# An LSTM over 512 steps: the x products of the last steps as one-level Strassen pairs, with the weight sums on GpSimd

## The chip, the cores and the metric

One core of one Trainium2 chip. The metric is the device time of the whole program in microseconds (us): median of three runs before the change 3068.2 us (3067.43 to 3068.24). One further execution was recorded by the hardware profiler; the traces below are of that one. Engines: PE is TensorE, DVE is VectorE, ACT is ScalarE, POOL is GpSimd, SP issues the DMAs.

## What is computed

```
xW = einsum('ntd,dg->ntg', x, Wx) + b           # x: 32 x 512 x 512, Wx: 512 x 2048
def step(carry, xw_t):
    a = xw_t + prev_h @ Wh                       # Wh: 512 x 2048
    i, f, o = sigmoid(first three quarters of a); g = tanh(last quarter)
    next_c = f * prev_c + i * g
    next_h = o * tanh(next_c)
out = x + hs
```

All of it is float32. Each of the 512 steps needs the h of the step before; the x products of a step need nothing of the recurrence and can be made at any earlier time.

## The kernel before

**A step.** The 32 rows of the batch sit in 32 of PE's columns, and four column groups (j = 0 to 3) work side by side on four quarters of the gates. `h_part` (line 544) multiplies h by Wh: in the steps up to 468 it takes 16 matmuls of 512 columns, from step 469 on (`SPLIT`) 32 of 256 columns, since the units are then treated as two halves. Its order in a split step is half 0 with the first two k, half 1 with the first k, half 0 with the last two, half 1 with the last three, where the first two k are the h of half 0, the last two that of half 1. So half 0 is complete after 20 of 32 matmuls. `cell` (line 557) then runs for each half: ACT takes the sigmoids and the tanh out of PSUM (`s`, `o`), DVE multiplies (`prod`), adds (`s`, which holds c), ACT takes tanh (`tanh_c`), DVE multiplies by o (`hbuf`) and transposes into `ht`, which the next step's matmuls read. The chain of half 0 is called chain A in the prediction. At the end of `cell` the residual sum `oc` (x plus h, 128 columns) is made on POOL, on DVE in the last eight steps. `seed_step` copies the x products of the next step into its PSUM banks on ACT, ahead of the step's `cell`.

**The x products.** Steps 0 to 17 are made early. The 480 steps 18 to 497 come in 15 groups of 32, through a fast scheme (26 block products for a 4x4 split, with a Strassen level inside each), whose block products are streamed between the h parts; DVE adds them up (`w_op`, 1024 columns each) and SP stores and reloads them through `xwd`. The last stream matmuls are in step 467; sums of the last group (`w_op`, one in a step) go on until step 476.

**The last 14 steps** (498 to 511) are plain products. For each step there are 16 units (four chunks of x times four quarters q of the columns); a unit is four matmuls of 128 columns, and two neighbouring units of a half are issued as four of 256. They fill PE behind the h part: 11 units in step 467, 13 in step 468, 5 in each of the steps 469 to 508, none in 509 to 511. When a step's 16 units are done, DVE adds the bias and moves the bank to SBUF (128x512). Lines 1240 to 1245 and 1395 to 1412 hold this; `plain_part` (line 485) issues one unit or two. The raw weights that they read are loaded again late (`late_loads`, steps 452 to 467).

The order of the instructions in steps 0 to 19 comes from a planner that lists recorded operations by due times; from step 20 on (`nc.flush()`) each engine gets its instructions in the order in which the code is written. An engine runs them in that order.

Of the kernel before, what the change touches and what calls it, by code (L numbers as in the profile page):

```python
# [13 lines left out]
P = 128  # L14
B = 32
T = 512
NJ = 4
# [4 lines left out]
W = G * P  # L22
HW = G * H

HEAD = 18
GS = 32
NG = 15
TAIL = T - HEAD - NG * GS
# [11 lines left out]
END = HEAD + GS * NG - AHEAD  # L40
SPLIT = END + 2
# [63 lines left out]
class Plan:  # L105
# [57 lines left out]
    def add(self, engine, op, call, out, ins):  # L163
        if not self.live:
            call()
            return
        self.ops.append((engine, op, call, out, ins))
# [219 lines left out]
def kernel(  # L387
# [10 lines left out]
    nc = Plan(tc.nc)  # L398
    add, sub = nc.vector.tensor_add, nc.vector.tensor_sub
# [6 lines left out]
    xbank = [psum.tile([P, W], F32, name=f"xbank_{i}") for i in range(5)]  # L406
# [24 lines left out]
    def buf_of(i):  # L431
        if i < NC:
            return cbuf[:, i]
        return spare if i == NC else r1[:, i - NC + 1]
# [22 lines left out]
    def x_plain(t):  # L457
        if 2 * TC <= t < HEAD:
            return xnat[:, 2, t % TC]
        return x_early[:, t % TC] if T - TAIL <= t < T - TC else x_of(t)  # L460
# [5 lines left out]
    def raw(blk):  # L466

        if late_weights[0]:
            return late_r[:, LATE_AT[blk]] if blk < 6 else late_more[blk - 6]
        return r1[:, blk]  # L470
# [14 lines left out]
    def plain_part(t, c, q, n, bank):  # L485

        ko, ki = divmod(c, 2)
        a = q % 2 * P
        for j in range(NJ):
            nc.tensor.matmul(  # L490
                bank[j * B : (j + 1) * B, q * P : (q + n) * P],
                x_plain(t)[:, c],
                raw(ko * 4 + j)[:, 2 * ki + 1 - q // 2, a : a + n * P],
                start=c == 0 and q == 0,
                stop=True,
                skip_group_check=True,
            )
# [121 lines left out]
    def take(pool):  # L619
        assert pool, "no buffer left"  # L620
        return pool.pop(0)
# [396 lines left out]
    xw_late = {}  # L1018
# [125 lines left out]
    def keep(p, bias_in=False):  # L1144
# [12 lines left out]
        if p >= PARKED:  # L1157
            kept_stores.append(lambda: nc.sync.dma_start(out=kept[n], in_=dst))

    with tc.manual_schedule():  # L1160
        nc.vector.memset(tanh_c, 0.0)
        nc.vector.memset(sring[0], 0.0)
# [74 lines left out]
        }  # L1237

        HEAD_STEPS = STREAM0
        plain_tail = []  # L1240
        tail_banks = [xbank[2], xbank[3]]
        for p in range(TAIL):
            plain_tail += [(p, c, q) for c in range(4) for q in range(4)]
        plain_tail[8:24] = plain_tail[16:24] + plain_tail[8:16]
        late_halves = []

        for p in HEAD_PLAINS[0]:
            nc.scalar.copy(plain_bank(p), bias_full)

        for t in range(T):  # L1250
# [141 lines left out]
                late_loads.pop(0)()  # L1392
            emit_matmuls(n)
            load_v_ahead()
            kept_late = []
            due = 0 if t < END else max(0, 13 - n // 2) if t < SPLIT else 5
            while due and plain_tail:
                p, c, q = plain_tail[0]
                m = 2 if due > 1 and q % 2 == 0 else 1
                plain_part(HEAD + NG * GS + p, c, q, m, tail_banks[p % 2])  # L1400
                del plain_tail[:m]
                due -= m
                if c == 3 and q + m == 4:
                    kept_late.append(p)
            cell(t)
            for p in kept_late:
                if not late_halves:
                    late = buf_of(take(free_c))
                    late_halves += [late[:, 0:2], late[:, 2:4]]
                dst = late_halves.pop(0).rearrange("p s c -> p (s c)")  # L1410
                xw_late[HEAD + NG * GS + p] = dst
                add(dst, tail_banks[p % 2], bias_full)
            if t == T - 8:
                nc.vector.transpose(x_last, x_of(T - 1).rearrange("p q b -> p (q b)"))

# [49 lines left out]
```

## Time and profile before

| what | value |
|---|---|
| median of three runs | 3068.2 us (3067.43 to 3068.24) |
| profiled execution | 3067.07 us, span 3065.3 us |
| PE busy | 3055.8 us (100%) |
| DVE busy | 2339.0 us (76%) |
| ACT busy | 1466.3 us (48%) |
| POOL busy | 248.4 us (8%), 504 `oc` sums of 483 ns in the mean |
| PE in the chain that ended last | 99% |
| granted PE clock | 1.000 |

Times in the trace are counted from the start of the span. A row of the timeline gives start, length, engine, operation, out<-in and shapes, and in brackets how long the engine stood idle before it and what ended that. A window row gives for each engine busy time and number of records, then granted clock, DMA share and GB/s. Nearly all instructions carry line 125, that of the recording layer, so the tiles tell them apart. A float32 matmul leaves two records.

### The profile page before, as it was taken

The numbers are of one execution on the slowest core, as the hardware profiler recorded it, in microseconds if no ns is written. First come the engines' busy times: TensorE is split into PE (matmuls) and PEld (weight loads), VectorE is DVE, ScalarE is ACT, GpSimd is POOL, SyncE is SP. The second block draws the span as 40 slices with busy tenths as digits, with TensorE's granted clock in tenths as the row PEclk, the third lists the DMA queues.
The fourth block names the chain that finished last, engine by engine and source line by source line (L and its number), as shares of the span: only waits on it lengthen the run. The fifth ranks groups of instructions, "written<-read, shape, count | busy, mean of one in ns | idle before, by whom it ended". The sixth has DMA issues, their size and how long they took to land.

```text
span 3065.3 us, 108321 instructions
## 1 busy us (share of the span) xinstructions
PE 3055.8 (100%) x43688; PEld 1614.1 (53%) x43688; DVE 2339.0 (76%) x6312; ACT 1466.3 (48%) x5474; POOL 248.4 (8%) x511
## 2 busy tenths in 40 slices
PE   9999999999999999999999999999999999999999
PEld 6774444444445555555555555555555555555676
DVE  8678787787878878787787877878778787787644
ACT  1345445454444544544445454454544445454444
POOL 1000000000000000000000000000000000000110
PEclk9999999999999999999999999999999999999999
DMA  9988887787877878778787777777877787788530
GB/s 329 328 283 281 266 258 256 239 263 235 267 245 247 262 238 269 241 245 268 233 272 236 247 265 240 256 251 246 262 245 254 245 257 256 235 271 269 158 87 18
DMA packets 320436, 752.61 MB, mean 246 GB/s; under 512 B 52160, under 2 KB 104640, under 8 KB 319424
## 3 DMA queue, kind: packets, MB, share of 16 engines
q1 hardware_dynamic: 319936, 745.69, 75.4%
q8 instruction: 344, 5.64, 0.8%
q14 instruction: 156, 1.28, 0.1%
HBM read 564.34 MB, written 184.30 MB: 244 GB/s over the span
## 4 chain that ended last, share of the span: by engine, by line
PE 99%; DVE 1%; DMA 0%; SPq 0%; ACT 0%; issue 0%; ACTq 0%; DVEq 0%
PE gbank L125 55%; PE xbank L125 38%; PE bbank L125 6%; DMA vdram<-vring 0%; DVE xs L125 0%; DMA xnat<-in_x_dram 0%; DVE ubuf L125 0%; SPq L125 0%; DVE prod L125 0%; ACT s L125 0%; DVE s L125 0%; DVE xbank L125 0%; DVE hbuf L125 0%; ACT tanh_c L125 0%; DVE ht L125 0%
## 5 line engine op out<-in xcount | busy, mean ns | idle before, releaser
L125 PE MATMUL gbank<-wh_sb,ht 128*32 128x512 f32 (+1 forms) x16256 | 1772.2, 575 | 1.7 <-DVE ht L125 1.6
L125 PEld LDWEIGHTS gbank<-wh_sb,ht 128*32 128x32 f32 x16256 | 588.6, 110 | 840.6 <-issue 711.6
L125 ACT ACTIVATE s<-gbank 128x64 f32<-128x64 f32 (+2 forms) x1920 | 331.2, 257 | 1211.3 <-PE gbank L125 1210.7
L125 PE MATMUL xbank<-vring,ubuf 128*32 128x256 f32 (+1 forms) x13584 | 848.1, 368 | 0.0
L125 PEld LDWEIGHTS xbank<-vring,ubuf 128*32 128x32 f32 x13584 | 513.1, 110 | 305.1 <-issue 137.3
L125 DVE TENSOR_TENSOR prod<-s 128x128 f32<-128x128 f32 (+1 forms) x1007 | 290.7, 289 | 486.5 <-ACT s L125 481.9
L125 POOL TENSOR_TENSOR oc<-xnat,ht 128x128 f32<-128x128 f32 x504 | 243.3, 483 | 2745.4 <-DVE ht L125 1360.1
L125 ACT ACTIVATE tanh_c<-s 128x64 f32<-128x64 f32 (+1 forms) x1007 | 259.1, 257 | 238.7 <-DVE s L125 236.4
L125 DVE STREAM_TRANSPOSE ht<-hbuf 128x64 f32<-128x64 f32 (+1 forms) x1005 | 247.5, 246 | 72.6 <-DVE hbuf L125 0.9
L125 ACT COPY cbuf<-xbank 128x256 f32<-128x256 f32 (+1 forms) x679 | 281.9, 439 | 40.2 <-PE xbank L125 33.1
L125 ACT COPY gbank<-xw 128x512 f32<-128x512 f32 (+1 forms) x486 | 285.1, 589 | 3.6 <-DMA vring<-vdram 2.5
L125 DVE TENSOR_TENSOR s<-prod 128x64 f32<-128x64 f32 (+1 forms) x1007 | 227.5, 226 | 34.2
L125 DVE TENSOR_TENSOR hbuf<-o,tanh_c 128x64 f32<-128x64 f32 (+1 forms) x1007 | 209.2, 208 | 34.5 <-ACT tanh_c L125 33.7
L125 DVE TENSOR_TENSOR cbuf<-xbank,cbuf 128x256 f32<-128x256 f32 x452 | 176.5, 409 | 48.5 <-ACT cbuf L125 43.4
L125 DVE TENSOR_TENSOR cbuf<-cbuf 128x1024 f32<-128x1024 f32 x172 | 209.5, 1222 | 0.7
L125 PE MATMUL xbank<-vring,r 128*32 128x256 f32 (+1 forms) x3216 | 207.5, 357 | 0.0
L125 PE MATMUL xbank<-vring,xs 128*32 128x256 f32 (+1 forms) x3120 | 200.8, 356 | 0.0
L125 PE MATMUL bbank<-vring,ubuf 128*32 128x256 f32 (+1 forms) x2600 | 183.2, 342 | 0.0
L125 ACT COPY r<-xbank 128x256 f32<-128x256 f32 (+1 forms) x411 | 175.1, 439 | 15.8 <-PE xbank L125 13.7
L125 PEld LDWEIGHTS xbank<-vring,r 128*32 128x32 f32 x3216 | 120.6, 110 | 81.3 <-issue 47.4
L125 ACT ACTIVATE o<-gbank 128x128 f32<-128x128 f32 (+1 forms) x508 | 154.7, 305 | 0.0
L125 PEld LDWEIGHTS xbank<-vring,xs 128*32 128x32 f32 x3120 | 115.8, 110 | 62.6 <-issue 23.5
(128 smaller groups left out, 2120.3 us busy)
## 6 DMA issues: line engine op xcount, KB each, us to landing
vring<-vdram SPq DMA_DIRECT2D x310, 896.0 KB, 5.9
xw<-xwd SPq DMA_DIRECT2D x1920, 64.0 KB, 4.5
xwd<-cbuf SPq DMA_DIRECT2D x140, 512.0 KB, 4.5
xwd<-r SPq DMA_DIRECT2D x83, 512.0 KB, 4.7
out_dram<-oc SPq DMA_DIRECT2D x255, 128.0 KB, 3.8
xnat<-in_x_dram SPq DMA_DIRECT2D x62, 512.0 KB, 5.3
xs<-in_x_grouped_dram SPq DMA_DIRECT2D x45, 512.0 KB, 5.0
vring<-vdram SPq DMA_DIRECT2D x33, 512.0 KB, 5.1
```

Source lines behind the costliest of these rows:

```text
L125: self.plan.add(self.name, op, lambda: call(*args, **kw), out, rest)
```

## The change

Steps 499 to 510 are taken as six pairs. A pair is a 2x2 block product for each half ko of the depth: rows are the two steps, the depth is cut into two chunks, the columns into two halves of 256. Seven products (Winograd's form of Strassen) replace eight. Each product has four units, so a pair has 28 units where two plain steps had 32. Steps 498 and 511 stay plain, 16 units each. In all there are 200 units instead of 224.

- **Weight sums**: t1 = b12 - b11, t2 = b22 - t1, t3 = b22 - b12, n4 = b21 - t2 for each of eight blocks of weights, 256 columns each; `prepare` issues 1024 columns a step on POOL in the steps 468 to 475. They go into `ubuf` and a part of `vring`, which the stream no longer needs.
- **Sums of x** (`begin`): four POOL operations of 64 columns for each pair; ACT also copies the bias seed into the pair's bank.
- **Results**: products accumulate in PSUM so that a pair needs four ACT copies (begin 512, corners 2x256, right 256, finish 256 columns) and three DVE adds (top, right, low, 256 columns each). They stand behind the `cell` of the step in whose fill their last unit was issued.
- **Order**: `fill` takes units until the step's share is reached, or until a product needs a copy that is not yet issued; `share` spreads the paired units up to step 507 and the rest up to step 509. Units by step: 467: 8; 468: 13; 469: 5; 470: 2; 471: 5; 472: 3; 473 to 488: 5 each; 489 to 509: 4 each; 510 and 511: none.

POOL, from the residual sum of step 467 to that of step 471; before, only residual sums stand there (ht_95 and ht_96 are the h of even and odd steps, oc_97 and oc_98 the two result buffers):

```order
L125 TENSOR_TENSOR oc_98<-xnat,ht_96 128x128
L125 TENSOR_TENSOR oc_97<-xnat,ht_95 128x128
L125 TENSOR_TENSOR oc_97<-xnat,ht_96 128x128
L125 TENSOR_TENSOR oc_98<-xnat,ht_95 128x128
L125 TENSOR_TENSOR oc_98<-xnat,ht_96 128x128
```

And now, from the end of step 467 to the residual sum of step 470 (xs_79, cbuf and r_74 hold the raw weights, ubuf and vring the sums, seeds_own the x of steps 496 to 503):

```order
L125 TENSOR_TENSOR vring<-seeds_own 128x64
L125 TENSOR_TENSOR vring<-vring,seeds_own 128x64
L125 TENSOR_TENSOR vring<-seeds_own 128x64
L125 TENSOR_TENSOR vring<-seeds_own,vring 128x64
L125 TENSOR_TENSOR ubuf<-xs_79 128x2x256 x2
L125 TENSOR_TENSOR oc_97<-xnat,ht_95 128x128
L125 TENSOR_TENSOR ubuf<-xs_79 128x2x256
L125 TENSOR_TENSOR ubuf<-cbuf 128x256
L125 TENSOR_TENSOR vring<-r_74 128x256
L125 TENSOR_TENSOR oc_97<-xnat,ht_96 128x128
L125 TENSOR_TENSOR ubuf<-xs_79,ubuf 128x2x256 x2
L125 TENSOR_TENSOR oc_98<-xnat,ht_95 128x128
```

The four small sums of x of the first pair come first; then each step has its weight sums ahead of its own residual sum and behind that of the step before.

PE in step 507, before: the h part, then five units of the plain product of step 511 (four units as eight matmuls of 256 columns, one as four of 128), then the h part of step 508 (xbank_66 and xbank_67 hold the two halves of odd steps, gbank those of even ones):

```order
L125 MATMUL xbank_66<-wh_sb,ht_95 32x256 x8
L125 MATMUL xbank_67<-wh_sb,ht_95 32x256 x12
L125 MATMUL xbank_69<-xs_79,xnat 32x256 x6
L125 MATMUL xbank_69<-cbuf,xnat 32x256
L125 MATMUL xbank_69<-r_74,xnat 32x256
L125 MATMUL xbank_69<-xs_79,xnat 32x128 x2
L125 MATMUL xbank_69<-cbuf,xnat 32x128
L125 MATMUL xbank_69<-r_74,xnat 32x128
L125 MATMUL gbank_72<-wh_sb,ht_96 32x256 x8
```

And now, the same place:

```order
L125 MATMUL xbank_66<-wh_sb,ht_95 32x256 x8
L125 MATMUL xbank_67<-wh_sb,ht_95 32x256 x12
L125 MATMUL xbank_68<-ubuf,xnat 32x256 x7
L125 MATMUL xbank_68<-vring,xnat 32x256
L125 MATMUL gbank_72<-wh_sb,ht_96 32x256 x8
```

The fill of step 507 is now the last product of the sixth pair, four units that read the sums in ubuf and vring; the fifth unit is gone.

DVE near the end, before: the residual sum of step 508, the bias sum of step 511 (the row with bias_full), and the first operations of the `cell` of step 509:

```order
L125 TENSOR_TENSOR oc_97<-xnat,ht_95 128x128
L125 TENSOR_TENSOR cbuf<-xbank_69,bias_full 128x512
L125 TENSOR_TENSOR prod<-s_90 128x128
L125 TENSOR_TENSOR s_89<-prod 128x64
L125 TENSOR_TENSOR hbuf<-o_91,tanh_c 128x64
L125 STREAM_TRANSPOSE ht_96<-hbuf 128x64
```

And now: the residual sum of step 509, the same bias sum, and the `cell` of step 510:

```order
L125 TENSOR_TENSOR oc_97<-xnat,ht_96 128x128
L125 TENSOR_TENSOR cbuf<-xbank_69,bias_full 128x512
L125 TENSOR_TENSOR prod<-s_89 128x128
L125 TENSOR_TENSOR s_90<-prod 128x64
L125 TENSOR_TENSOR hbuf<-o_91,tanh_c 128x64
L125 STREAM_TRANSPOSE ht_95<-hbuf 128x64
```

The bias sum of step 511 stood behind the residual sum of step 508 and now stands behind that of step 509; ACT's copies that seed step 511 are in the same place in both, ahead of the `cell` of step 510.

The core of the diff (methods that only pick an operand are left out):

```diff
-            kept_late = []
-            due = 0 if t < END else max(0, 13 - n // 2) if t < SPLIT else 5
-            while due and plain_tail:
-                p, c, q = plain_tail[0]
-                m = 2 if due > 1 and q % 2 == 0 else 1
-                plain_part(HEAD + NG * GS + p, c, q, m, tail_banks[p % 2])
...
+            if t >= SPLIT - 1:
+                tail.prepare(1280)
+            done = tail.fill(0 if t < END else max(0, 13 - n // 2) if t < SPLIT else tail.share(t))
             cell(t)
...
+            for f in done:
+                f()
```

```diff
+        def prepare(self, cols):
+            while self.making and self.making[0][2] * HW <= cols:
+                kind, blk, k = self.making.pop(0)
+                cols -= k * HW
+                z, w = self.raw_of(blk, k), self.sum_of(blk, k)
+                b12, b11, b22, b21 = (z[:, :, i] for i in range(4))
+                t1, t2, t3, n4 = (w[:, :, i] for i in range(4))
+                nc.gpsimd.tensor_sub(*((t1, b12, b11), (t2, b22, t1), (t3, b22, b12), (n4, b21, t2))[kind])
...
+        def begin(self, n):
...
+            nc.scalar.copy(self.banks[n % 3], self.seed)
+            a, b = (x_plain(t).rearrange("p (k i) b -> p k i b", i=2) for t in self.steps(n))
+            s1, s2, s3, s4 = (self.sums[:, n % 2, i] for i in range(4))
+            nc.gpsimd.tensor_add(s1, b[:, :, 0], b[:, :, 1])
+            nc.gpsimd.tensor_sub(s2, s1, a[:, :, 0])
+            nc.gpsimd.tensor_sub(s3, a[:, :, 0], b[:, :, 0])
+            nc.gpsimd.tensor_sub(s4, a[:, :, 1], s2)
...
+        def top(self, n):
+            t = self.results[n]
+            add(t[:, 0], bbank[:, n % 2 * HW : (n % 2 + 1) * HW], t[:, 0])
+
+        def right(self, n):
+            self.done.add(("right", n))
+            t, bank = self.results[n], self.banks[n % 3]
+            nc.scalar.copy(t[:, 1], bank[:, 0:HW])
+            add(t[:, 1], bank[:, HW:W], t[:, 1])
...
+        def share(self, t):
+            gone = self.total - len(self.units)
+            if gone < self.paired:
+                return -(-(self.paired - gone) // max(1, T - 4 - t))
+            return -(-(self.total - gone) // max(1, T - 2 - t))
```

More of the change, by code (lines that the diff above doesn't have):

```diff
@@ L1239 @@
         HEAD_STEPS = STREAM0
[L1240 to L1245, printed above, removed]
+        tail = Tail()
         for p in HEAD_PLAINS[0]:
@@ L1394 @@
             load_v_ahead()
-            kept_late = []
-            due = 0 if t < END else max(0, 13 - n // 2) if t < SPLIT else 5
-            while due and plain_tail:
-                p, c, q = plain_tail[0]
-                m = 2 if due > 1 and q % 2 == 0 else 1
-                plain_part(HEAD + NG * GS + p, c, q, m, tail_banks[p % 2])
[L1401 to L1404, printed above, removed]
-            cell(t)
[L1406 to L1412, printed above, removed]
+            if t >= SPLIT - 1:
+                tail.prepare(1280)
+            done = tail.fill(0 if t < END else max(0, 13 - n // 2) if t < SPLIT else tail.share(t))
+            cell(t)
+            for f in done:
+                f()
             if t == T - 8:
```

138 lines of the change are left out of this document (added).

## The prediction

> **What bounds the kernel now.** First the head of the page, then the windows view over the stretch that the change touches, then PE's waits from 2850 us on.
>
> ```profile
> span 3065.3 us, 108321 instructions
> PE 3055.8 (100%) x43688; PEld 1614.1 (53%) x43688; DVE 2339.0 (76%) x6312; ACT 1466.3 (48%) x5474; POOL 248.4 (8%) x511
> 2866.82:3048.22 181.40, 181.40 (x3525) 130.71 (x3521) 91.47 (x344) 84.24 (x397) 20.62 (x36) 1.00 0.25 75
> PE xbank L125 <- DVE ht L125: 0.8, 1, 0.8
> PE gbank L125 <- DVE ht L125: 0.7, 1, 0.7
> ```
>
> The third row is the window from the start of step 469 to the start of step 509: 40 steps in 181.40 us, 4.535 us each, PE busy all of it at clock 1.00. In the whole tail PE waits twice, 1.5 us in all. So PE bounds these steps, and matmuls taken away count, until the recurrence takes over. That happens at the end, where no x products are left (PE in order of time; a float matmul leaves two records, so x64 are the 32 matmuls of one h part):
>
> ```profile
> 2984.72 3.66 PE L125 MATMUL xbank<-wh_sb,ht 128*32 128x256 f32 x64
> 2989.26 3.66 PE L125 MATMUL gbank<-wh_sb,ht 128*32 128x256 f32 x64
> 3034.82 3.45 PE gbank L125 x64
> 3052.20 0.26 DVE ht L125
> 3048.22 3.66 PE L125 MATMUL xbank<-wh_sb,ht 128*32 128x256 f32 x64
> 3052.59 3.66 PE L125 MATMUL gbank<-wh_sb,ht 128*32 128x256 f32 x64 [0.71 <-DVE ht L125]
> 3057.03 3.66 PE L125 MATMUL xbank<-wh_sb,ht 128*32 128x256 f32 x64 [0.78 <-DVE ht L125]
> ```
>
> With five units of x product, 2984.72 to 2989.26 is 4.54 us. The h part alone holds PE 3.45 us (third row, from the chain of waits; the fourth is from there too: an ht that ends at 3052.46 and PE's start at 3052.59, 0.13 us later), so a unit costs (4.535 - 3.45) / 5 = 0.217 us. With no units, steps 509 and 510 still take 4.37 and 4.44 us: **the floor of the recurrence is about 4.41 us, and PE's five units stand only 0.125 us above it.** That decides what the saved matmuls are worth.
>
> Now one step (472, from 2880.42), so that the free room on DVE, ACT and POOL is seen:
>
> ```profile
> 2880.42 3.66 PE L125 MATMUL gbank<-wh_sb,ht 128*32 128x256 f32 x64
> 2880.71 0.26 ACT L125 ACTIVATE tanh_c<-s 128x64 f32<-128x64 f32 x1 [0.60 <-DVE s L125]
> 2880.89 0.68 ACT L125 COPY xbank<-xw 128x256 f32<-128x256 f32 x2
> 2881.26 0.24 DVE L125 STREAM_TRANSPOSE ht<-hbuf 128x64 f32<-128x64 f32 x1
> 2881.43 1.18 DVE L125 TENSOR_TENSOR cbuf<-cbuf,r 128x1024 f32<-128x1024 f32 x1
> 2881.65 1.28 POOL L125 TENSOR_TENSOR oc<-xnat,ht 128x128 f32<-128x128 f32 x1 [3.99 <-DVE ht L125]
> 2882.85 0.39 ACT L125 ACTIVATE s<-gbank 128x128 f32<-128x128 f32 x2 [1.27 <-PE gbank L125]
> 2883.27 0.29 DVE L125 TENSOR_TENSOR prod<-s 128x128 f32<-128x128 f32 x1 [0.66 <-ACT s L125]
> 2883.60 0.23 DVE L125 TENSOR_TENSOR s<-prod 128x64 f32<-128x64 f32 x1
> 2883.86 0.26 ACT L125 ACTIVATE tanh_c<-s 128x64 f32<-128x64 f32 x1 [0.50 <-DVE s L125]
> 2884.14 0.23 DVE L125 TENSOR_TENSOR hbuf<-o,tanh_c 128x64 f32<-128x64 f32 x1 [0.32 <-ACT tanh_c L125]
> 2884.51 0.25 DVE L125 STREAM_TRANSPOSE ht<-hbuf 128x64 f32<-128x64 f32 x1
> ```
>
> Chain A, of the first half of the units, starts +2.43 us into the step and needs three DVE operations with two SBUF inputs: prod (+2.85), s (+3.18), hbuf (+3.72, to +3.95). POOL's residual sum (oc) takes 1.28 us and ends at +2.51.
>
> **The change, part by part.**
>
> *Matmuls.* 224 units become 200. Counted from the order of both kernels: step 467 drops from 11 to 8 units, 468 keeps 13, 469, 471 and 473 to 488 keep 5, 470 has 2, 472 has 3, 489 to 508 have 4 instead of 5, 509 has 4 instead of none. A plain count would give 24 x 0.217 = 5.2 us. The floor cuts it: four units need 3.45 + 0.87 = 4.32 us, under 4.41. So steps 489 to 508 give 20 x 0.125 = **-2.5 us** (floor 4.37 to 4.44: -1.9 to -3.3), and step 509 costs nothing. Step 467 is not split, and its h comes late:
>
> ```profile
> 2854.34 3.64 PE L125 MATMUL gbank<-wh_sb,ht 128*32 128x512 f32 x32
> 2859.72 0.24 DVE L125 STREAM_TRANSPOSE ht<-hbuf 128x64 f32<-128x64 f32 x1
> 2860.57 0.64 PE L125 MATMUL gbank<-wh_sb,ht 128*32 128x512 f32 x4
> ```
>
> Three units less would let step 468 begin 0.65 us earlier than 2860.57, but the first half of ht ends at 2859.96, and 0.13 us later PE can begin, at 2860.09: **-0.5 us**.
>
> *The weight sums on GpSimd.* In each of steps 468 to 475 POOL gets 1024 columns: two sums of 512 in the even steps, one of 512 and two of 256 in the odd ones. They stand behind oc of the step before, which waits for ht, so they start where chain A starts. The trace has such POOL sums once, in the head, beside DVE:
>
> ```profile
> 32.74 0.95 DVE L125 TENSOR_TENSOR ubuf<-cbuf 128x768 f32<-128x768 f32 x1
> 33.61 0.42 DVE L125 TENSOR_TENSOR vring<-cbuf 128x256 f32<-128x256 f32 x1
> 34.55 0.91 DVE L125 TENSOR_TENSOR ubuf<-cbuf 128x256 f32<-128x256 f32 x1
> 35.38 2.04 DVE L125 TENSOR_TENSOR xs<-r,ubuf 128x768 f32<-128x768 f32 x1
> 37.34 2.03 DVE L125 TENSOR_TENSOR xs<-cbuf,ubuf 128x768 f32<-128x768 f32 x1
> 33.66 1.52 POOL L125 TENSOR_TENSOR xw<-xw,bias_full 128x512 f32<-128x512 f32 x1 [33.22 <-ACT xw L125]
> 35.14 3.42 POOL L125 TENSOR_TENSOR cbuf<-cbuf,bias_full 128x512 f32<-128x512 f32 x2
> 2877.20 0.46 POOL L125 TENSOR_TENSOR oc<-xnat,ht 128x128 f32<-128x128 f32 x1 [3.28 <-issue]
> ```
>
> Beside POOL a 768-column operation takes 2.04 and 2.03 us instead of 0.95, a 256-column one 0.91 instead of 0.42. The ends show turns: POOL's first sum ends at 35.18, DVE's 256 columns at 35.46; DVE's first 768 end at 37.42, POOL's third sum at 38.56, DVE's next 768 at 39.37. Each engine stands still until the other's operation is over. In step 472 oc loses likewise: 1.28 us behind DVE's 1024 columns against 0.46 alone (last row). From these ends: a 512-column sum holds DVE 38.56 - 37.42 = 1.14 us, 128 columns hold it 2882.93 - 2882.61 = 0.32 us, so by a line through both 256 columns hold 0.59 and 64 hold 0.18 us (estimates). A DVE operation that waited ends 0.14 us sooner after its release than its whole length (0.81 for 0.95): prod 0.15, s and hbuf 0.09.
>
> Now step 472 again. oc ends +2.51, the first sum takes over by +2.60 (0.1 us between POOL operations, estimated from 0.46 less 0.32) and holds to +3.74. prod, due at +2.85, ends at +3.89 instead of +3.14. The second sum has been waiting since before, takes its turn, and holds s to +5.03; s ends at +5.12 instead of +3.41: chain A is 1.71 us late, and the next step starts at 4.37 + 1.71 = 6.08 instead of 4.535: +1.55. In an odd step the second sum frees s at +4.48 (s ends +4.57), and the third holds hbuf to +5.16, end +5.25 instead of +3.95: 4.37 + 1.30 = 5.67, +1.14. Step 468 has 13 units of cover and loses about nothing. So three even steps (470, 472, 474) and four odd ones: 3 x 1.55 + 4 x 1.14 = **+9.2 us**. The fewer units of 470 and 472 gain nothing there, since PE waits anyway.
>
> If s may go ahead of the second sum, the turn falls on hbuf: in an even step the sum holds from +3.98 to +5.12 and hbuf ends at +5.21, 1.26 late, +1.10; in an odd step hbuf ends about 0.88 late, +0.71; sum 3 x 1.10 + 4 x 0.71 = +6.1. Below that only no contention at all, 0 us. I take +9.2, since in the head DVE's 768 columns were issued at 35.38, before the running 256 ended at 35.46, and yet POOL's sum went first.
>
> What a page adds to that: the Trainium skill, "SBUF — State Buffer", section "Who interferes with whom", says that a DVE instruction with two SBUF inputs and a GpSimd one that reads SBUF cannot overlap, and that the order of issue decides who stands still. The head rows agree (2.04 for 0.95). By that rule the second sum, waiting before s is issued, goes first, which is the +9.2; the +6.1 would need DVE to be preferred, and a kernel whose sums stood on DVE would not pay it at all.
>
> PE's own need of the sums is covered: each kind is complete a step before the unit that reads it, by the spare 3.45 us of an h part.
>
> *Small sums and copies.* Each pair adds four 64-column POOL sums (4 x 0.28 = 1.1 us; after an undisturbed oc, that ends +1.77 in a step like the one of the last row, to about +2.9, just on prod): at most 0.2 us, swallowed by the 0.125 of the five-unit steps, about +0.2 in the two pairs that fall later. In step 473 they push the three big sums onto the second half's chain instead, for which I charge the same 1.14. ACT gets four copies a pair:
>
> ```profile
> L125 ACT COPY cbuf<-xbank 128x256 f32<-128x256 f32 (+1 forms) x679 | 281.9, 439 | 40.2 <-PE xbank L125 33.1
> L125 ACT COPY gbank<-xw 128x512 f32<-128x512 f32 (+1 forms) x486 | 285.1, 589 | 3.6 <-DMA vring<-vdram 2.5
> L125 DVE TENSOR_TENSOR cbuf<-xbank,cbuf 128x256 f32<-128x256 f32 x452 | 176.5, 409 | 48.5 <-ACT cbuf L125 43.4
> 3049.61 0.68 DVE L125 TENSOR_TENSOR cbuf<-xbank,bias_full 128x512 f32<-128x512 f32 x1
> ```
>
> At most 0.44 + 0.59 = 1.03 us fall into one step, and ACT is free from +1.15 (end of the 0.68 us of copies) to +2.43: 1.28 us. Cost nothing; without that room up to 0.4 us in each of six steps. The three DVE adds a pair (0.41) fit between ht at +1.08 and prod: 1.08 + 0.41 + 1.18 = 2.67. No DMA is added or moved on SP.
>
> *The last plain step.* Its bias sum (0.68, ends +2.07 after 3048.22) moves from behind step 508 to behind 509; the two copies (0.68) that seed step 511 wait for it on ACT, ahead of step 510's first sigmoid: ready at +2.75 instead of +2.43, **+0.3 us**.
>
> **Sum.** -2.5 - 0.5 + 9.2 + 0.2 + 0.3 = +6.7 us. The profiled execution took 3067.07 us (span 3065.3 and 1.8 around it), so 3073.8; the median of the runs is 3068.2, 1.1 above it, so I forecast **3074.9 us**, 0.22% slower.
>
> **Rivals.**
> - *The sums hide.* DVE's short operations slip in between and the chain loses less than its 0.125 us a step: -2.5 - 0.5 + 0.5 = -2.5, 3065.7 us, not slower. For it: the change's 1024 columns a step (2.3 us of POOL) fit a 4.5 us step. Against it: the three slow DVE rows of the head. It decides if prod and s keep 0.29 and 0.23 us beside sums. 0.20.
> - *PE is all that counts.* The full 5.2 us: 3063.0. Against it: 4.37 and 4.44 us with no units at all. 0.03.
> - *The second half is held as well.* If the sums start later than +2.9, the last is still running when the second half's prod is due (about +4.15 plus the delay), and each of seven steps pays one more hold of 0.59 to 1.14 us, 0.86 in the mean: +6, 3080.9. For it: a DVE add ahead of the 1024 columns, and the small sums of step 473. 0.14.
> - *It doesn't save matmuls.* Excluded: 24 units fewer stand in PE's order.
>
> **How the numbers follow.** The forecast case, 0.63, runs from +3.6 (turns the other way, 6.1) to about +9: 3071.8 to 3077. A change of 0.2% is 6.1 us, about what a measurement of this kernel tells from no change: the line lies at 3074.3, and 0.37 of the 0.63 above it. Slower: 0.37 + 0.14 = 0.51. Same: 0.26 + 0.20 + 0.03 - 0.01 = 0.48. Faster by 6.1 us is more than all 24 units are worth: 0.01. The range takes in the first rival and most of the third: 3065.2 to 3080.
>
> **What would show it.** Right: in steps 469 to 475 PE idles 0.7 to 1.6 us before each h part, behind DVE's ht; prod, s or hbuf last over 1 us there, beside POOL sums of 512; steps 489 to 508 take about 4.41 us with 0.1 us of idle PE; 476 to 488 stay at 4.535. Wrong: prod and s at their old lengths beside the sums, or PE waiting for POOL itself, or four-unit steps of 4.32 us.

## The result and the profile after

The changed kernel takes 3078.44 us (median of six runs, 3077.04 to 3079.25), the kernel before, in the same comparison, 3068.02 us (3067.38 to 3068.35). The ratio is 1.0034, 95% interval 1.0021 to 1.0047: 10.4 us slower. A second comparison, the last of the experiments, gave 3077.76 against 3067.69 us and the same ratio (1.0021 to 1.0046).

The head of the page of the changed kernel, and PE's waits from 2850 us on:

```profile
span 3076.9 us, 108025 instructions
PE 3056.4 (99%) x43504; PEld 1576.2 (51%) x43504; DVE 2349.7 (76%) x6319; ACT 1475.3 (48%) x5499; POOL 278.1 (9%) x555
```

```profile
PE xbank L125 <- DVE ht L125: 6.9, 4, 2.2
PE gbank L125 <- DVE ht L125: 3.7, 4, 1.3
PE xbank L125 <- DVE hbuf L125: 0.4, 1, 0.4
```

184 matmul records are gone, and PE is busy 0.6 us longer all the same; half speed for 3.5 us, shown below, is a part of that. Where it waited 1.5 us in the tail it now waits 11.0. The windows show the stretch. First the steps 468 to 475 (time span, length, then PE, PEld, DVE, ACT and POOL busy, clock, DMA share, GB/s), of the kernel before, then of the changed one with its steps 489 to 508 as a second row:

```profile
2860.57:2898.56 37.99, 37.99 (x712) 26.36 (x708) 24.46 (x72) 16.11 (x77) 7.74 (x8) 1.00 0.45 138
```

```profile
2860.65:2910.73 50.08, 40.26 (x683) 24.59 (x681) 36.51 (x74) 18.49 (x85) 34.31 (x36) 0.97 0.34 107
2969.72:3059.01 89.29, 89.28 (x1604) 53.65 (x1600) 41.05 (x173) 46.03 (x211) 9.64 (x24) 1.00 0.14 42
```

Eight steps take 12.1 us more. PE has 29 records fewer in them, DVE two operations more, yet DVE is "busy" 12.05 us longer: waiting time inside its operations. The twenty later steps take 89.29 us, 4.465 each instead of 4.535: 1.4 us less.

One step in detail: 470, from 2872.64, to be compared with step 472 of the prediction. DVE first, then POOL:

```profile
2875.49 1.14 DVE L125 TENSOR_TENSOR prod<-s 128x128 f32<-128x128 f32 x1 [0.57 <-ACT s L125]
2876.66 1.17 DVE L125 TENSOR_TENSOR s<-prod 128x64 f32<-128x64 f32 x1
2878.15 0.22 DVE L125 TENSOR_TENSOR hbuf<-o,tanh_c 128x64 f32<-128x64 f32 x1 [0.32 <-ACT tanh_c L125]
```

```profile
2873.90 1.35 POOL L125 TENSOR_TENSOR oc<-xnat,ht 128x128 f32<-128x128 f32 x1 [1.83 <-DVE ht L125]
2875.20 2.54 POOL L125 TENSOR_TENSOR ubuf<-xs,ubuf 128x512 f32<-128x512 f32 x2
```

`prod` starts 2.85 us into the step, as before, and takes 1.14 us instead of 0.29; `s` takes 1.17 instead of 0.23. They are exactly the two operations that overlap POOL's two sums. `s` ends at +5.19 us (the prediction had +5.12, before it was +3.41), and the next h part waits 2.17 us for `ht`. PE's h parts of steps 471 to 474, with their waits in brackets (start, length):

```profile
2878.90 3.66 PE L125 MATMUL xbank<-wh_sb,ht 128*32 128x256 f32 x64 [2.17 <-DVE ht L125]
2884.94 3.67 PE L125 MATMUL gbank<-wh_sb,ht 128*32 128x256 f32 x64 [1.29 <-DVE ht L125]
2891.27 5.35 PE L125 MATMUL xbank<-wh_sb,ht 128*32 128x256 f32 x64 [2.02 <-DVE ht L125]
2898.51 3.66 PE L125 MATMUL gbank<-wh_sb,ht 128*32 128x256 f32 x64 [0.81 <-DVE ht L125]
```

One row stands out: the h part of step 473 (2891.27) is 5.35 us long where the others are 3.66. Its window has the reason, the clock (third number from the end):

```profile
2891.27:2894.79 3.52, 3.52 (x36) 2.33 (x40) 2.34 (x6) 1.62 (x5) 2.12 (x4) 0.52 0.35 104
```

PE ran at half speed for 3.5 us, right after three steps in which it had waited 1.3 to 2.2 us each. The last experiment is about this.

From row to row the starts give a table of the whole difference, in us (the second column is a second profile of the changed kernel, from the last experiment):

| stretch | prediction | changed kernel | second profile |
|---|---|---|---|
| up to step 467 | 0 | +0.54 | -0.06 |
| step 467 (6.23 before) | -0.5 | -0.46 | -0.45 |
| steps 468 to 475 (37.99) | +9.2 | +12.09 | +10.77 |
| steps 476 to 488 (58.95) | +0.2 | +0.04 | +0.04 |
| steps 489 to 508 (90.71) | -2.5 | -1.42 | -1.40 |
| step 509 (4.37) | 0 | +0.09 | +0.10 |
| step 510 (4.44) | +0.3 | +0.38 | +0.38 |
| from step 511 to the end | 0 | +0.34 | +0.32 |
| sum | +6.7 | +11.60 | +9.70 |

### The profile page after: what moved, and what is told of

The parts are those of the page before. It is cut to its first block, busy times and chain, and to the rows that moved or that the text cites. A ratio compares the mean times of both kernels' runs of the same rounds, so it can differ in the third digit from the quotient of the medians.

```text
span 3076.9 us, 108025 instructions
## 1 busy us (share of the span) xinstructions
PE 3056.4 (99%) x43504; PEld 1576.2 (51%) x43504; DVE 2349.7 (76%) x6319; ACT 1475.3 (48%) x5499; POOL 278.1 (9%) x555
## 4 chain that ended last, share of the span: by engine, by line
PE 96%; DVE 1%; DMA 1%; ACT 0%; SPq 0%; issue 0%; DVEq 0%; ACTq 0%
PE gbank L125 55%; PE xbank L125 36%; PE bbank L125 6%; DMA bias_full<-in_L_cond_b_dram 0%; DMA r<-in_L_cond_Wx_dram 0%; DVE prod L125 0%; DVE s L125 0%; DMA xwd<-xnat 0%; SPq L125 0%; DVE ubuf L125 0%; ACT s L125 0%; DVE hbuf L125 0%; DMA seeds_at<-in_L_cond_b_dram 0%; DVE ht L125 0%; ACT tanh_c L125 0%
## 5 line engine op out<-in xcount | busy, mean ns | idle before, releaser
L125 PEld LDWEIGHTS gbank<-wh_sb,ht 128*32 128x32 f32 x16256 | 578.1, 110 | 858.6 <-issue 716.2
L125 PEld LDWEIGHTS xbank<-vring,ubuf 128*32 128x32 f32 x13584 | 504.1, 110 | 314.1 <-issue 138.5
L125 ACT COPY cbuf<-xbank 128x256 f32<-128x256 f32 (+1 forms) x694 | 288.7, 440 | 40.9 <-PE xbank L125 34.4
```

The source lines that it names most:

```text
L125: self.plan.add(self.name, op, lambda: call(*args, **kw), out, rest)
```

## The experiments

The theory: POOL's sums and the recurrence's DVE operations read through something that only one of them can use at a time, so each sum stands in the chain with its whole length. The rivals: the pairs' copies and adds on ACT and DVE lengthen the chain; or POOL's activity as such does; or PE waits for the sums themselves. Each kernel is the changed one with the edit shown, unless it says otherwise. A row with steps 468 to 475 is always the same window view as above. Where only one run was made, small differences of the whole time tell little (the part before step 467, which no edit touches, ended between 2853.97 and 2856.60 us); the stretch tells more.

### Without the weight sums

```diff
-            return self.sum_of(blk, 1)[:, 0, {5: 0, 6: 1, 7: 2, 4: 3}[r]]
+            return raw(blk)[:, {5: 0, 6: 1, 7: 2, 4: 3}[r]]
...
-                tail.prepare(1280)
+                tail.prepare(0)
```

The weight sums are left out, and the products read raw blocks in their place; copies, adds, small sums and the order of PE stay.

> The changed kernel with the weight sums left out: the products that should read a sum read one raw block of weights instead, all else stays (matmuls, small sums of x, copies, adds). Theory A (DVE operations with two SBUF inputs and POOL's sums stand still for each other, on the recurrence): the steps 468 to 475 go back from 50.1 us to about 38.0, and the whole from 3078.4 to about 3066.3 us. Rival B (the pairs' copies and adds on ACT and DVE, or PE's waits for operands, make the loss): it stays above 3074 us.

```profile
2860.68:2898.66 37.98, 37.42 (x684) 23.75 (x685) 25.46 (x75) 19.13 (x85) 11.52 (x16) 1.00 0.45 140
```

3066.31 us (before, in the same series: 3067.47). Steps 468 to 475 take 37.98 us, as in the kernel before, with all of the pairs' copies and adds in place. So those cost next to nothing here, and the 12.1 us come with the sums. The rest of the change saves time: steps 489 to 508 take 4.466 us each here too.

### The sums alone, in the kernel before

The kernel before, with the same POOL operations at the same places, and nobody reads them.

```diff
...
+            if t >= SPLIT - 1:
+                prepare(1280)
             kept_late = []
```

> The kernel before, with the same weight sums added on POOL in the steps 468 to 475, and nothing that reads them: no pairs, no copies, no adds. Theory A: the steps 468 to 475 take about 50 us as in the changed kernel, and the whole about 3068.0 + 12 = 3080 us. Rival B: no loss, 3068 us.

```profile
2862.77:2911.34 48.57, 39.45 (x712) 24.51 (x705) 36.09 (x72) 15.31 (x77) 31.62 (x28) 1.00 0.36 110
```

3079.88 us, 12.4 over the kernel before (2.2 of it ahead of step 467, which started at 2856.53 instead of 2854.34); the eight steps take 48.57, +10.6, at clock 1.00. No product reads the sums here, so PE does not wait for them: the sums slow the recurrence as bystanders. Step by step it is 6.24, 5.38, 6.27, 6.09, 6.28, 5.94, 6.50, 5.87 us, in steps 470 and 472 within 0.05 us of the changed kernel's; its step 474, at 6.50, is 0.22 longer, and why was not looked for.

### POOL writes only

```diff
-                nc.gpsimd.tensor_sub(*((t1, b12, b11), (t2, b22, t1), (t3, b22, b12), (n4, b21, t2))[kind])
+                nc.gpsimd.memset((t1, t2, t3, n4)[kind], 0.0)
```

The sums are left out and zeros written to their places, with as many POOL instructions of the same output shapes.

> The changed kernel with POOL only writing zeros where the weight sums belong (no reading; the products then read zeros). Theory A in the form that only POOL's reads of SBUF keep DVE out: prod, s and hbuf keep 0.29, 0.23 and 0.23 us, the whole about 3066.5 us. Theory A in the form that any running POOL instruction keeps DVE out: DVE waits as long as a memset runs; a 512-column memset may be shorter than a sum, so the loss shrinks with its length, but prod or s still show some tenths of a us more.

DVE and POOL in its step 470:

```profile
2876.01 0.29 DVE L125 TENSOR_TENSOR prod<-s 128x128 f32<-128x128 f32 x1 [0.60 <-ACT s L125]
2876.33 0.22 DVE L125 TENSOR_TENSOR s<-prod 128x64 f32<-128x64 f32 x1
...
2875.66 0.99 POOL L125 MEMSET ubuf<- 128x512 f32 x2
```

```profile
2862.38:2900.35 37.97, 37.42 (x683) 23.75 (x684) 25.45 (x74) 19.14 (x85) 19.10 (x36) 1.00 0.49 147
```

`prod` runs from 2876.01 to 2876.30 while POOL writes (2875.66 to 2876.65), and takes 0.29 us; the eight steps take 37.97. The whole, 3068.24 us, is over what was expected only by what came before step 467 (2856.60 against 2854.91 in the kernel without sums). The memsets are also shorter (0.99 us for two, against 2.54), so that alone would shrink a hold; but a hold of half a memset would still show on a 0.29 us operation, and there is none. POOL's activity as such is excluded: it is its reading.

### Smaller pieces

```diff
-            blocks = ((0, 2), (2, 2), (4, 2), (6, 1), (7, 1))
+            blocks = tuple((blk, 1) for blk in range(8))
...
-                tail.prepare(1280)
+                tail.prepare(1024)
```

The same sums in pieces of 256 columns, four a step.

> The changed kernel with every weight sum in pieces of 256 columns, four in each of the steps 468 to 475, the same columns in all. Theory A: a DVE operation waits for one piece at most, 0.6 us instead of 1.14, so chain A loses about 0.75 us in a step, a step about 0.6 us, and some of the second half's chain is held too; the whole 3071 to 3074 us. A rival by which only POOL's whole time counts: 3078 us or a little more, since four operations cost more than two.

DVE and POOL in its step 470:

```profile
2875.80 0.59 DVE L125 TENSOR_TENSOR prod<-s 128x128 f32<-128x128 f32 x1 [0.57 <-ACT s L125]
2876.43 0.64 DVE L125 TENSOR_TENSOR s<-prod 128x64 f32<-128x64 f32 x1
2877.40 0.36 DVE L125 TENSOR_TENSOR hbuf<-o,tanh_c 128x64 f32<-128x64 f32 x1 [0.32 <-ACT tanh_c L125]
...
2875.51 2.84 POOL L125 TENSOR_TENSOR ubuf<-xs,ubuf 128x256 f32<-128x256 f32 x4
```

3073.90 us; steps 468 to 475 take 45.36. Now three operations are held instead of two, `s` by 0.41 us instead of 0.94. As many columns cost 7.4 us instead of 10.8 to 12.1: what counts is how many turns the chain meets and how long each is, not the columns.

### The sums on DVE

```diff
-                nc.gpsimd.tensor_sub(*((t1, b12, b11), (t2, b22, t1), (t3, b22, b12), (n4, b21, t2))[kind])
+                nc.vector.tensor_sub(*((t1, b12, b11), (t2, b22, t1), (t3, b22, b12), (n4, b21, t2))[kind])
```

> The changed kernel with the weight sums on DVE at the same place in the program, instead of on POOL. Theory A: no waits between the engines, but the sums stand in DVE's own order between the 1024-column sum and prod; prod starts about 0.7 us late in the steps 469 to 475, a step takes about 5.05 us instead of 6.2, the whole 3069 to 3071 us. Rival: the place, not the engine, is what costs, and it stays at 3076 us or more.

Its step 470 on DVE:

```profile
2874.14 1.55 DVE L125 TENSOR_TENSOR ubuf<-xs,ubuf 128x512 f32<-128x512 f32 x2
2875.62 0.28 DVE L125 TENSOR_TENSOR prod<-s 128x128 f32<-128x128 f32 x1
2875.93 0.22 DVE L125 TENSOR_TENSOR s<-prod 128x64 f32<-128x64 f32 x1
```

3073.18 us, 2.2 over the upper end of what was expected; the eight steps 44.32, +6.3. Steps 471, 473 and 475 took 5.67, 6.20 and 5.78 us where 5.05 was expected, and step 467 began 1.1 us later than in the kernel before. The two sums take 1.55 us on DVE, of which the idle 0.6 ahead of `prod` hides a part, and nothing is held afterwards. So the same sums on the very engine whose chain is at stake are 4.4 to 5.8 us cheaper than beside it.

### The chain's operands in PSUM

If the sums hold DVE operations with two SBUF inputs, operations with one input in PSUM must run at their old length beside them. In steps 469 to 475 ACT writes the sigmoids into the unused half of the step's gate bank, and `prod` becomes two multiplications of 64 columns (shortened):

```diff
-                nc.scalar.activation(s[:, u, 0:2], g[:, n_, 0:2], AF.Sigmoid)
+                up = PAIRS[(t - SPLIT) % 2][u][:, HW:W].rearrange("p (k u) -> p k u", u=H)
+                nc.scalar.activation(up[:, 0:2], g[:, 0, 0:2], AF.Sigmoid)
...
-                nc.vector.tensor_mul(prod[:, u], s[:, u, 0:2], s[:, u, 2:4])
-                add(nxt[:, u, 3], prod[:, u, 0], prod[:, u, 1])
+                nc.vector.tensor_mul(prod[:, u, 1], up[:, 1], s[:, u, 3])
+                nc.vector.tensor_mul(up[:, 0], up[:, 0], s[:, u, 2])
+                add(nxt[:, u, 3], up[:, 0], prod[:, u, 1])
```

> The changed kernel, all of its work kept, but in the steps 469 to 475 the chain's DVE operations read one operand from PSUM: ACT writes the sigmoids of i, f and o into the unused half of the gate bank, and prod is two operations of 64 columns, f*c and i*g. Theory A (only two SBUF inputs stand still beside POOL): the steps 469 to 475 lose at most 0.1 us each, the 0.6 us of step 468 stay, the whole about 3067.5 us. Rival B, and a rival C by which any DVE operation waits for a running POOL sum: 3077 to 3079 us.

DVE, POOL and ACT in its step 471:

```profile
2882.29 0.23 DVE L125 TENSOR_TENSOR prod<-xbank,s 128x64 f32<-128x64 f32 x1 [0.36 <-ACT xbank L125]
2882.55 0.23 DVE L125 TENSOR_TENSOR xbank<-xbank,s 128x64 f32<-128x64 f32 x1
2882.82 0.23 DVE L125 TENSOR_TENSOR s<-xbank,prod 128x64 f32<-128x64 f32 x1
...
2880.81 2.26 POOL L125 TENSOR_TENSOR ubuf<-xs,ubuf 128x512 f32<-128x512 f32 x1
...
2881.50 0.26 ACT L125 ACTIVATE xbank<-xbank 128x128 f32<-128x128 f32 x1 [0.67 <-PE xbank L125]
2881.80 0.22 ACT L125 ACTIVATE s<-xbank 128x64 f32<-128x64 f32 x1
2882.05 0.21 ACT L125 ACTIVATE xbank<-xbank 128x64 f32<-128x64 f32 x1
```

The time is a miss: 3074.40 us where 3067.5 was expected. The mechanism is not. Three DVE operations take 0.23 us each between 2882.29 and 2883.05, inside POOL's 512-column sum (2880.81 to 2883.07); in the changed kernel such a place cost 0.94 us. What the expectation had not counted is the chain's own new length: ACT's three operations start 0.25 to 0.30 us apart and take 0.76 us, against 0.51 for the same three in the kernel before (2869.24 to 2869.75), and there is one DVE operation more. The steps 470 to 475 take 5.29 us each.

A control has the same chain and no sums (the edit of the first experiment on top of this one; the weight sums are left out).

```diff
-                tail.prepare(1280)
+                tail.prepare(0)
```

> The control of the run e3_psum_chain: the same PSUM operands in the steps 469 to 475, but the weight sums left out (products read raw blocks). If the 5.29 us of a step in e3_psum_chain are the longer chain itself (three ACT operations in a row, a late second half) and not POOL, the steps 469 to 475 keep 5.29 us and the whole is 3073.8 us, 0.6 less than there because step 468 is free of sums. If sums still cost there: 3068 us.

It takes 3072.78 us, and 5.29 us in each of the same steps: the 5.29 is the chain's own, and in those steps the sums add nothing to it. A second attempt, with the sums, has the sigmoids go into the other bank, so that ACT reads one and writes the other:

```diff
-                up = PAIRS[(t - SPLIT) % 2][u][:, HW:W].rearrange("p (k u) -> p k u", u=H)
+                up = PAIRS[(t + 1 - SPLIT) % 2][u][:, HW:W].rearrange("p (k u) -> p k u", u=H)
```

> As e3_psum_chain, all work kept, but ACT writes the sigmoids into the unused half of the next step's gate bank instead of the bank it reads, so that its three operations need not wait for each other. Theory A: the steps 469 to 475 take 4.5 to 4.7 us, step 468 keeps its 0.6 us, the whole 3067 to 3068.5 us, about the time of the kernel before. Rival (POOL's sums still hold the chain): 3074 us or more.

3072.78 us, again a miss: ACT's three operations take 0.51 us again, and the steps still 5.08 us, 0.55 over the 4.535 of before. The rows show two pieces of that. The h part takes 3.88 us instead of 3.66, so that the first sigmoid of step 470 starts 2.72 us into the step instead of 2.43, and the one DVE operation more adds 0.26. Why the h part is longer stays open; in the two kernels above, with and without sums, it takes 3.94. So PSUM operands remove the contention (shown twice) and are no remedy here.

### The floor

The kernel before, with no units at all from step 473 on; their products are left out.

```diff
-            due = 0 if t < END else max(0, 13 - n // 2) if t < SPLIT else 5
+            due = 0 if t < END else max(0, 13 - n // 2) if t < SPLIT else 5 if t < SPLIT + 4 else 0
```

> The kernel before, with no x units from step 473 on; the products of those steps are left out. It tells what the floor of the recurrence is in many steps in a row. If 4.465 us, what the steps with four units take in the changed kernel, is the recurrence alone, the steps 477 to 508 take 4.46 to 4.47 us each here. If the four units or the pairs' copies and sums lengthen them over the floor of 4.41 that the prediction took from two steps, they take 4.37 to 4.43 here.

Steps 489 to 508 as one window, then the h parts of steps 473 and 474 and the last two on PE:

```profile
2957.04:3047.00 89.96, 73.31 (x1281) 40.30 (x1282) 38.51 (x166) 42.38 (x200) 7.31 (x16) 1.00 0.13 41
```

```profile
2885.29 3.66 PE L125 MATMUL xbank<-wh_sb,ht 128*32 128x256 f32 x64
2889.77 3.67 PE L125 MATMUL gbank<-wh_sb,ht 128*32 128x256 f32 x64 [0.81 <-DVE ht L125]
3051.45 3.66 PE L125 MATMUL gbank<-wh_sb,ht 128*32 128x256 f32 x64 [0.79 <-DVE ht L125]
3055.91 3.67 PE L125 MATMUL xbank<-wh_sb,ht 128*32 128x256 f32 x64 [0.79 <-DVE ht L125]
```

With nothing beside the h part, PE waits 0.8 us in each step, and a step takes 4.48 us (89.96 / 20 = 4.498 with one step of 4.83); the whole is 3065.93 us. It is 4.48 from the first such step on: 473, right behind a step with five units, runs from 2885.29 to 2889.77. That is a little over what either expectation had, and on the side of the recurrence: the four units do not lengthen the 4.465 us steps, and 4.41 was too low.

### Sums that are loaded

The sums can also come from elsewhere. The head makes t1, t2, t3 and n4 of six of the eight blocks for its own scheme and stores them; this kernel loads them by DMA, makes the other two blocks' sums on DVE in step 468, and gives step 468 11 units.

```diff
-                nc.gpsimd.tensor_sub(*((t1, b12, b11), (t2, b22, t1), (t3, b22, b12), (n4, b21, t2))[kind])
+                for blk in stored:
+                    nc.sync.dma_start(out=self.sum_of(blk, 1)[:, 0, 0], in_=vdram[stored[blk], :, 1])
+                for blk in (2, 4):
+                    for op in ((t1, b12, b11), (t3, b22, b12), (t2, b22, t1), (n4, b21, t2)):
+                        sub(*op)
...
```

> The weight sums of six of the eight blocks are no longer made on GpSimd: the head had made the same sums for the fast scheme and stored them, so they are loaded by DMA in the steps 468 to 473. Those of the two other blocks are made on DVE in step 468, where it stands idle for 3.3 us. Step 468 has 11 units instead of 13. The theory (only GpSimd's reads beside DVE's chain cost the time, the saved matmuls are there) expects prod at 0.29 and s at 0.23 us in steps 469 to 475, PE without waits there, steps 468 to 475 in about 37.5 us (5.85 for step 468, 31.7 for the seven others) instead of 50.1, steps 489 to 508 still at 4.465 each, and the whole at 3066.2 us, 1.8 under the kernel before (3065.5 to 3067). The rival (the sums come late whichever way they come, since loads of DMA must land in time, or DVE's eight sums in step 468 hold its own chain) expects PE to wait for ubuf or vring in steps 469 to 475, or step 468 at 7 us or more, and the whole at 3068 or over.

3066.43 us (11 runs) against 3067.63, ratio 0.9996, interval 0.9987 to 1.0005. Steps 469 to 475 are back at 4.46 to 4.63 us without a wait for the loads. Step 468 is not as expected: 6.85 us, since the eight sums on DVE end at 2865.01, and `prod` was due at 2863.87 (ACT's first sigmoid starts at 2863.44, and in the kernel before `prod` follows it by 0.43 us):

```profile
2864.14 0.87 DVE L125 TENSOR_TENSOR ubuf<-xs,ubuf 128x256 f32<-128x256 f32 x2
2864.93 0.28 DVE L125 TENSOR_TENSOR prod<-s 128x128 f32<-128x128 f32 x1
```

The next kernel spreads the eight: four in step 468, two in 469, one each in 470 and 472 (kind 0 to 3 for t1, t2, t3, n4, with the block).

```diff
-                for blk in (2, 4):
-                    for op in ((t1, b12, b11), (t3, b22, b12), (t2, b22, t1), (n4, b21, t2)):
-                        sub(*op)
+            own = {SPLIT - 1: ((0, 2), (0, 4), (1, 2), (1, 4)), SPLIT: ((2, 2), (2, 4)), SPLIT + 1: ((3, 2),), SPLIT + 3: ((3, 4),)}
+            for kind, blk in own.get(t, ()):
+                sub(*((t1, b12, b11), (t2, b22, t1), (t3, b22, b12), (n4, b21, t2))[kind])
```

> The kernel with the stored sums, with the eight sums that DVE makes itself spread: four in step 468, two in step 469, one each in steps 470 and 472, where DVE stands idle 0.6 to 0.8 us between its 1024 columns and prod. Theory: the step 468 of the kernel before this one took 6.85 us because the eight sums ended 0.7 us after prod was due; with four it takes 5.85, the steps 469 to 475 stay at 4.45 to 4.65, 468 to 475 take 37.6 us, and the whole 3065.4 us (3064.8 to 3066.5), some 2.2 to 2.6 under the kernel before. Rival: step 468 is long for another reason (PE's first matmul with half of h waited for DVE's hbuf, which stood behind both halves' sigmoids), and stays at 6.2 or more: 3065.8 to 3066.4; or a sum in step 469 or 470 holds prod, and that step takes 4.8 or more.

```profile
2863.26 1.00 DVE L125 TENSOR_TENSOR ubuf<-xs,ubuf 128x256 f32<-128x256 f32 x2
2864.59 0.29 DVE L125 TENSOR_TENSOR prod<-s 128x128 f32<-128x128 f32 x1 [0.32 <-ACT s L125]
```

3066.00 us (11 runs, 3065.02 to 3066.51) against 3067.85: ratio 0.9993, interval 0.9984 to 1.0002. Step 468 takes 5.80 us, the eight steps 37.54, and from the start of step 467 to that of step 511 it is 201.14 us against 202.69 before and 213.41 in the changed kernel. It is 12 us under the changed kernel; that it is also under the kernel before, by 1.5 us in the stretch and 1.85 in the medians, is within what the comparison leaves open.

### The changed kernel once more

Nothing is edited.

> The changed kernel, unaltered. In its profiled execution the granted clock falls to 0.52 for 3.5 us at the start of step 473, and that h part takes 5.14 us instead of 3.45: 1.7 us of the step's 7.24. The kernel with the sums alone has no such dip there (its dip is at 8 to 11 us from the start), though PE waits as long. If the dip is chance, it isn't at step 473 in a second profile: step 473 takes 5.4 to 6.0 us, steps 468 to 475 take 48 to 48.9 us together instead of 50.1, runs without a dip lie at 3076.5 to 3077.5, and a run in five or so has a mean clock of 0.999, as among those of the kernel before. If PE's waits of 1.3 to 2.2 us in the steps ahead bring it on, it comes again between steps 470 and 475, and most runs have a mean clock of 0.999 and lie at 3078 to 3079.5.

3077.76 us (six runs, 3076.80 to 3079.54) against 3067.69. In its profile the half clock is there again, in step 471, and not in 473. Three windows: the dip, then steps 473 and 474.

```profile
2879.75:2883.05 3.30, 3.30 (x37) 2.16 (x37) 2.25 (x4) 0.78 (x4) 3.30 (x4) 0.52 0.02 5
2890.76:2895.33 4.57, 4.57 (x88) 2.78 (x89) 3.58 (x11) 2.82 (x12) 3.17 (x6) 1.00 0.38 126
2895.33:2902.88 7.55, 4.95 (x96) 2.74 (x89) 6.10 (x10) 2.02 (x10) 5.96 (x6) 1.00 0.41 125
```

This dip cost almost nothing: steps 471 and 472 take 12.43 us together, 12.37 in the first profile, since PE had a wait of 2.02 us ahead of step 473 (now 1.90) and one of 1.29 ahead of 472 (now none) to lose it in. In the first profile the dip fell on step 473: steps 473 and 474 take 13.52 us there, 12.12 here, so it cost 1.4 us. That is the difference between the two sums of steps 468 to 475 (50.08 and 48.76, 1.3). Of the two expectations the second is borne out in its place (between steps 470 and 475 again), and less in its times: the mean clock is 0.999 in eight of the twelve runs of the changed kernel and 1.000 in four, and the former are 1.1 us longer in the mean (3078.56 against 3077.45). Among 40 runs of the kernel before in the last three series it is 0.999 in four. A mean does not tell where the dip lies: the kernel with the sums alone has 0.999 too, and its dip (0.54) lies 7.5 to 11.2 us from the start, behind waits of at most 1.05 us. In the steps 469 to 475 it waited 0.6 to 1.75 us each time and kept clock 1.00; in both profiles of the changed kernel the step of the dip began behind a wait of over 2 us (2.02 and 2.17), but the 2.17 us ahead of step 471 in the first profile had no dip behind it. So the waits may make the dip more likely; that is an argument from place and counts, and what sets it off was not tried.

## Why the prediction came out as it did

The forecast was +6.7 us on the profiled execution and 3074.9 us in all; it was 9.7 to 11.6 and 3077.8 to 3078.4. The mechanism was right, and so was the sign of each large term. The size of the sums' cost, step 468 and the saving of steps 489 to 508 were off, and the clock was in no term. The median lies above the 3071.8 to 3077 of the forecast case; the whole range, to 3080, took it in through a rival (the second half held as well) that came true in one step only, so that part is luck.

**The weight sums (+9.2 forecast, +10.8 measured without a paid dip, +12.1 with one).** The turns fell as the head's rows had them: the second sum went ahead of `s` (1.17 us) and `hbuf` stayed free (0.22), so the alternative of +6.1 is out. The Trainium skill, "SBUF — State Buffer", section "Who interferes with whom", agrees in both its halves: a DVE instruction with two SBUF inputs is held (1.14 for 0.29 us), and one that meets a GpSimd instruction which only writes is not (0.29 beside the memsets). In the three even steps the forecast was 6.08 us each and 6.26 to 6.33 was measured, 0.1 of it because the working added the delay to 4.37, the lowest value of the floor. The odd steps came out on both sides of 5.67: 5.17 in step 469, 5.94 to 6.22 in 471 and 475. In step 469 the sum of 512 columns had 0.32 us to go when `prod` began (2870.64 and 2870.32), in step 471 of the first profile 1.15 us (2882.91 and 2881.76).

One step of the working failed outright: "Step 468 has 13 units of cover and loses about nothing": it lost 0.57 us. The four small sums on POOL ahead of the big ones put the second of these on the chain:

```profile
2865.16 1.19 DVE L125 TENSOR_TENSOR s<-prod 128x64 f32<-128x64 f32 x1
...
2863.70 2.57 POOL L125 TENSOR_TENSOR ubuf<-xs 128x512 f32<-128x512 f32 x2
```

`s` took 0.96 us longer, and the cover was 0.40 us: in the kernel before the first half of `ht` ended at 2866.29, PE needed it at 2866.82, and 0.13 lie between. The kernel with the sums alone, which has no small sums, bears this out: there the two big sums end at 2866.46, ahead of `prod` (2866.96), `s` takes 0.23 us, and step 468 takes 6.24. And one term was missing, the clock: 1.4 us in one profile and about none in the other.

**Step 473** went as described, but is only seen in the second profile: the small sums pass (`prod` 0.33 us, the step 4.57), the big ones then hold the second half, and step 474 pays (7.55). Both together 12.12 us, where 5.67 + 6.08 = 11.75 was forecast. The rival in which the second half is held in all seven steps did not come; step 473 is its one case.

**Steps 489 to 508 (-2.5 forecast, -1.4 measured).** The step of the working that failed is the floor, read from steps 509 and 510 alone (4.37 and 4.44): without units a step takes 4.48. The two were short behind `hbuf`. `prod` starts at +2.85 us in step 509 as in step 473 of the kernel without units, `hbuf` at +3.72 and +3.73; but the transposition into `ht` starts 0.26 us after `hbuf` in step 509 (3051.94 to 3052.20), 0.33 in step 510, and 0.36 in that step 473 (2889.02 to 2889.38). What sets this gap was not looked for. The saving is 0.07 us a step, not 0.125. Of the 0.1 us of idle PE that was to show there, the trace shows nothing (PE 89.28 busy of 89.29); the ends of matmuls are modelled, and presumably cover such a gap.

**Small terms.** Step 467 gave 0.46 us (0.5 forecast). Step 510 lost 0.38 (0.3); the rows name what was predicted, the bias sum on DVE, then the seed's copies, then the first sigmoid at +2.88 us instead of +2.43:

```profile
3064.96 0.68 DVE L125 TENSOR_TENSOR cbuf<-xbank,bias_full 128x512 f32<-128x512 f32 x1
3065.73 0.68 ACT L125 COPY xbank<-cbuf 128x256 f32<-128x256 f32 x2 [1.63 <-DVE cbuf L125]
3066.35 0.38 ACT L125 ACTIVATE s<-gbank 128x128 f32<-128x128 f32 x2
```

The 0.2 us for small sums in the later pairs did not appear (+0.04), and copies and adds at nothing were right, as the kernel without the weight sums shows. The 0.3 us behind the start of step 511 was in no term. It lies behind the last DVE operation, where only the stores of the result are left: from its end (3062.70, now 3073.94) to the end of the span it is 2.6 us before and 3.0 now. Why was not looked for, nor was the cause of single steps of 4.7 to 4.8 us in some experiments.

## What to carry to other kernels

Before moving work to an idle engine, look what it shares with the engines of the critical chain: GpSimd was idle over 90% of the time, and 8192 columns of sums on it cost 11 to 12 us, on the busy DVE 6, and nothing that the eight steps show once most were loaded from where they already lay. Where two engines take turns, count how many operations of the chain meet a turn and how long the longest turn is, and allow for a clock that may fall when PE starts to wait. And a floor is to be read from a long stretch in which it binds, not from two steps.

## What the runs showed of the hardware

- **A half clock with waits of 2 us and less.** Granted clock 0.52 for 3.3 to 3.5 us in both profiles of the changed kernel, while PE was busy 40.1 to 40.3 us of the eight steps' 49 to 50 and waited up to 2.2 us at a time; 0.54 for 3.7 us near the start of the kernel with the sums alone, behind waits of up to 1.05 us. The Trainium skill, "TensorE: Matmul & The Clock Gate", section "HAM oscillation — how this bites in real kernels", has half the clock when PE idles for longer than about 3.4 us; the half agrees, but no wait in these stretches is longer than 2.2 us.
- **What a turn costs.** A 512-column float32 sum of two SBUF operands on POOL takes 1.25 us where DVE's chain has operands in PSUM, and in the changed kernel's even steps adds 0.85 to 0.95 us to the 64- or 128-column DVE operation of the chain that meets it; pieces of 256 add 0.30 to 0.41 to `prod` and `s`.
- **ACT from and to one PSUM bank.** Three activations that read one half of a bank and write its other half, or SBUF, start 0.25 to 0.30 us apart; where they write to another bank, 0.10 to 0.20 us. Whether the chip or waits in the program set this was not looked for.
